# Moving the last hidden rows and weight loads one loop forward, and reordering products, silus, statistics and head sums, in an attention and expert block

## The chip, the core and the metric

The kernel runs on one core of one Trainium2 chip. Its time is the device time of one execution in microseconds (us). Matmuls run on TensorE (PE in the profile; its weight loads are PEld), elementwise work on VectorE (DVE), activations and copies on ScalarE (ACT), some sums and all indirect DMAs on GpSimd (POOL); SyncE (SP) issues most other DMAs.

## The reference, cut to what matters

The input is x, 16 batches of 512 tokens with 256 columns. Biases are left out here:

```python
xn = layernorm(x)
q, k, v = fmap(xn @ Wq), fmap(xn @ Wk), xn @ Wv      # fmap(y) = elu(y) + 1, 16 heads of 16
att = ((q @ (k.T @ v)) / (q . sum(k))) @ Wo          # by batch and head
shared = (silu(xn @ w_in_a) * (xn @ w_in_b)) @ w_out # w_in, w1: 256 -> 2 x 512
h = silu(xn @ w1_a) * (xn @ w1_b)
routed = sum(p[e] * h @ w2[e] for e in best_two(xn)) # two of 8 experts, of one group of 4
out = x + att + shared + routed
```

## The kernel before, in words

One loop handles one batch b (512 tokens, 4 tiles of 128). All its matmuls are in fp32 but those of the sorting. An order written in Python is given to a scheduler, which places the instructions of each engine. It follows the order of the code, dependencies and the buffers of the pools; `tc.keep_in_program_order`, `tc.issue_after` and `tc.high_priority` bind it further.

In loop b the kernel does the following, each named by its function:

- `front(b + 1)` projects the next batch: pk (keys and routing scores) and pq (queries) are matmuls, then come biases, the feature map (min or Relu, and Exp, L324 to L328) and the routing, many small VectorE steps.
- `summarize` makes pxk = xn.T k, 8 matmuls; `normalize(b + 2)` makes the statistics (L285, L287), the Sqrt (L289) and the normalized rows of the batch after the next, sends them to DRAM and back and transposes them to xnT. Sqrt, Exp and Silu need three different tables on ScalarE, and each change is a table load (ACT_TABLE_LOAD).
- `hidden_rows(b)` makes the rows h for the experts (tiles phr and hr) and stores them to DRAM (h_d). `hidden(b)` makes the same for the shared expert, transposed (tiles phs and hs_all). Both call `seven`: for each half u it forms two sums of products out of 7 products, Strassen's way, from four sums of tokens (`token_sums`, tile ss). A product (u, i) is one matmul of 512 columns in phr and two of 256 in phs. Products add up in three PSUM tiles a half: tall, wide and lone. Product 1 is copied to r1 (L493), 6 and 7 to b1 and b2 (L496, L499), wide after 5 is added to b2 (L500), lone after 2 to r1 (L502), wide after 3 to b1 (L505). Then silu(r1) * b1 (L503, L506) and silu(tall) * b2 (L509, L510) are the outputs. r1 and the silu of tall (sa) share the pool tag "sa" of two buffers: r1 of half 0, r1 of half 1, sa 0, sa 1, then r1 of the next call. There are six PSUM buffers "mm" and two "py".
- `key_sum(b + 1)` and `attend(b + 1)` make the sum of keys (POOL, L602; matmul pks), and divide the queries by the normalizer (qk L658, rz L660 to L664, q*rz L665). `mix(b)` makes pvk (4 matmuls), vk (L637, L642), pm and kvo.
- `gather(b)` makes po for four token tiles: 4 matmuls with hs_all and w_out, 2 with kvo and the queries. It adds po to res and stores it to h_d (L695, L696).

The loop before the last (b = 14) also begins `order`, the sorting of all tokens by their pair of experts. It is a generator, advanced by `next(steps_of_order)` at places written by hand: slots for all tokens (L712 to L753), then eight groups of marks on VectorE (L770 x_all, L775 at_tile, L779 and L783) with 8 small matmuls (pi) each. Loop 14 takes 1 + 1 + 1 + 6 steps and loop 15 8 steps in its `hidden_rows` and the last.

The last loop (b = 15) begins with `token_sums` and `hidden_rows(15)`. Only after these is the place of w1's blocks free, and 16 DMAs of 128 KB load the last four experts' weights there (L198). Then the first rows are gathered from h_d by indirect DMA (L836) in the sorted order and turned: for a pair of tiles, 12 ScalarE copies to hb (L857, behind the silu of the half), 4 transposes of 32 partitions and 3 of 128 (L863, L869) give hT. 67 sorted tiles follow, four matmuls of 512 columns each (L886, tile py), then scatters, and the output tiles of batch 15.

Of the kernel before, what the change touches and what calls it, by code (L numbers as in the profile page):

```python
# [10 lines left out]
FP = mybir.dt.float32  # L11
AF = mybir.ActivationFunctionType
ALU = mybir.AluOpType
AX = mybir.AxisListType

P = 128
# [5 lines left out]
def block_kernel(  # L22
# [29 lines left out]
    nc = tc.nc  # L52
# [196 lines left out]
    ahead_of = keep.tile([P, TT + 1, NP], BF)  # L249
    nc.gpsimd.memset(ahead_of[:, 0, :], 0.0)  # L250

    last_xn, last_copy = [], []

    def turn(to, rows, tag, b, parts):

# [12 lines left out]

        return place

    def normalize(b):

        xt = xs[b]
        st = small.tile([P, NT, 6], FP, tag="st", name=f"st_{b}")
        mv = small.tile([P, NT, 2], FP, tag="mv", name=f"mv_{b}")
        sd = small.tile([P, NT], FP, tag="sd", name=f"sd_{b}")
        rs = small.tile([P, NT], FP, tag="rs", name=f"rs_{b}")
        xn = xn_all[:, b % 2]

        n = 1 if b == 0 else NT  # L280
        made = []
        for g in range(0, NT, n):
            with tc.issue_after(last_xn[-1].ins) if last_xn else nullcontext():
                for t in range(g, g + n):
                    nc.vector.bn_stats(out=st[:, t, :], in_=xt[:, t, :])  # L285
            for t in range(g, g + n):
                nc.vector.bn_aggr(out=mv[:, t, :], in_=st[:, t, :])  # L287
            with tc.issue_after(last_copy[-1].ins) if last_copy else nullcontext():
                nc.scalar.activation(sd[:, g : g + n], mv[:, g : g + n, 1], AF.Sqrt, bias=eps_sb)  # L289
            nc.vector.reciprocal(rs[:, g : g + n], sd[:, g : g + n])  # L290
            for t in range(g, g + n):
                made.append(nc.vector.tensor_scalar(
                    xn[:, t, :], xt[:, t, :], mv[:, t, 0:1], rs[:, t : t + 1],
                    ALU.subtract, ALU.mult,
                ))
        last_xn[:] = made[-1:]
        xnT = work.tile([P, KD, S], FP, tag="xnT", name=f"xnT_{b}")
        if b < 2:
            for t in range(NT):
                pt = ps_mm.tile([P, KD, P], FP, tag="mm", name=f"pt_{b}_{t}")  # L300
                for c in range(KD):
                    nc.tensor.transpose(
                        pt[:, c, :], xn[:, t, :].rearrange("p (m c) -> p c m", c=KD)[:, c], ident
                    )
                last_copy.append(nc.scalar.copy(xnT[:, :, ts(t, P)], pt))
            return xn, xnT, None
        last_copy.clear()
        nc.sync.dma_start(out=xn_d[b % 2].rearrange("(t p) d -> p t d", p=P), in_=xn)
        return xn, xnT, turn(xnT, xn_d[b % 2], "xb", b, "(i c)")
# [9 lines left out]
    def feature_map(b, y, tag):  # L319

        low = one.tile([P, NT, D], FP, tag="low", name=f"{tag}_{b}")
        if tag == "km":
            nc.vector.tensor_scalar(low, y, 0.0, None, ALU.min)  # L323
            nc.scalar.activation(low, low, AF.Exp)  # L324
        else:
            nc.scalar.activation(low, y, AF.Relu, scale=-1.0)
            nc.scalar.activation(low, low, AF.Exp, scale=-1.0)
        nc.vector.scalar_tensor_tensor(y, y, 0.0, low, ALU.max, ALU.add)  # L328

    def project(b, xnT):  # L330
# [128 lines left out]
    def token_sums(b, xnT):  # L459

        (x11, x12), (x21, x22) = halves(xnT)
        ss = one.tile([P, 4, S // 2], FP, tag="ss", name=f"ss_{b}")
        s1, s2, s3, s4 = (ss[:, i, :] for i in range(4))
        nc.vector.tensor_tensor(s1, x21, x22, ALU.add)
        nc.vector.tensor_tensor(s2, s1, x11, ALU.subtract)
        nc.vector.tensor_tensor(s3, x11, x21, ALU.subtract)
        nc.vector.tensor_tensor(s4, x12, s2, ALU.subtract)
        return [x11, x12, s4, x22, s1, s2, s3]

    def seven(name, product, view, room, done, then):  # L470
# [11 lines left out]
            )  # L482
        r1, b1, b2 = [None] * 2, [None] * 2, [None] * 2
        for n, (u, i) in enumerate((
            (0, 1), (0, 5), (1, 1), (0, 6), (1, 5), (1, 6), (0, 7), (0, 2), (1, 7), (0, 4), (0, 3),
            (1, 2), (1, 3), (1, 4),
        )):
            to = lone[u] if i == 2 else wide[u] if i in (3, 5) else tall[u]
            product(to, u, i - 1, i in (1, 2, 5), i in (2, 3, 4))
            with tc.high_priority():  # L490
# [5 lines left out]
                    nc.scalar.copy(b1[u], view(tall[u]))  # L496
                elif i == 7:
                    b2[u] = room(u, 1)
                    nc.scalar.copy(b2[u], view(tall[u]))  # L499
                    nc.vector.tensor_tensor(b2[u], b2[u], view(wide[u]), ALU.add)  # L500
                elif i == 2:
                    nc.vector.tensor_tensor(r1[u], r1[u], lone[u], ALU.add)  # L502
                    nc.scalar.activation(r1[u], r1[u], AF.Silu)  # L503
                elif i == 3:
                    nc.vector.tensor_tensor(b1[u], b1[u], view(wide[u]), ALU.add)  # L505
                    done(u, 0, None, nc.vector.tensor_tensor(b1[u], view(r1[u]), b1[u], ALU.mult))  # L506
# [92 lines left out]
    def key_sum(b, kk):  # L599

        k2 = one.tile([P, 2, D], FP, tag="k2", name=f"k2_{b}")
        nc.gpsimd.tensor_tensor(k2, kk[:, 0:2, :], kk[:, 2:4, :], ALU.add)  # L602
        nc.gpsimd.tensor_tensor(k2[:, 0, :], k2[:, 0, :], k2[:, 1, :], ALU.add)
        pks = ps_y.tile([P, D], FP, tag="py", name=f"pks_{b}")
        nc.tensor.matmul(pks, lhsT=ones, rhs=k2[:, 0, :], start=True, stop=True)
# [14 lines left out]
        nc.scalar.copy(xk, pxk)  # L620
        return xk

    def mix(b, xk, ksb):

        pvk = ps_mm.tile([P, KD, P], FP, tag="mm", name=f"pvk_{b}")
        for c in range(KD):
            for k in range(KD):
                nc.tensor.matmul(
# [6 lines left out]
        with tc.high_priority():  # L635
            for c in range(KD):
# [5 lines left out]
            nc.vector.tensor_tensor(  # L642
                vk, vk, headmask.unsqueeze(1).to_broadcast([P, KD, P]), ALU.mult
            )
        pm = ps_mm.tile([P, KD, D], FP, tag="mm", name=f"pm_{b}")
        for c in range(KD):
            nc.tensor.matmul(
# [40 lines left out]

    def gather(b, res, qT, kvo, hs, placed, then):

        for t in range(NT):
            po = outputs(b, t, qT, kvo, hs)

            with tc.issue_after(placed.ins) if placed and t > 1 else nullcontext():
                nc.vector.tensor_tensor(res[:, t, 0:D], po, res[:, t, 0:D], ALU.add)  # L695
            nc.sync.dma_start(out=h_d[ts(b * NT + t, P), HID:ROW], in_=res[:, t, :])  # L696
            between(b, then(t))

    def order():

# [221 lines left out]
    for b in range(B):  # L922
        xn, xnT, _ = normed.pop(b)
        res, qq, kk = fronts.pop(b)
        if b + 1 < B:
            fronts[b + 1] = front(b + 1, normed[b + 1][1])
        if b + 2 == B:
# [3 lines left out]
            )  # L931
            steps_of_order = order()
        if b + 1 == B:
            sums7 = token_sums(b, xnT)
            hidden_rows(b, sums7, {2: 2, 6: 2, 9: 2, 13: 2}.get)

            for e in waiting:
                load_expert(e)
            *lists, filled = next(steps_of_order)
            tiles = [Tiles(list(range(i, min(i + 2, SURE))), *lists) for i in range(0, SURE, 2)]  # L940
        xk = summarize(b, xn, kk)
# [14 lines left out]
        if b + 1 < B:  # L956
            sums = key_sum(b + 1, fronts[b + 1][2])
            queries[b + 1] = attend(b + 1, fronts[b + 1][1], sums)
        if b + 2 == B:
            next(steps_of_order)  # L960
        if b + 1 == B:
# [1 line left out]
                w.rows()  # L963
        hs, made = hidden(b, sums7) if b else first_hidden(xnT)
        if b + 1 < B:
            kvo = mix(b, xk, ksb)
        if b + 2 == B:
            next(steps_of_order)
        if b + 1 < B:
            gather(b, res, qT, kvo, hs, normed[b + 2][2]() if b + 2 < B else None, {0: 2, 1: 2, 3: 2}.get)  # L970

# [10 lines left out]
    for g, w in enumerate(tiles):  # L982
# [3 lines left out]
            tiles[g + AHEAD - 1].turn()  # L986
        w.sums()
        if g == AHEAD:
            kvo = mix(B - 1, xk, ksb)

    def rest(i):
        if i < TILES:
# [59 lines left out]
```

## Time and profile before

| | |
|---|---|
| median of 3 runs | 1048.22 us (1044.43 to 1048.23) |
| the profiled execution | 1048.47 us, span 1046.7 us |
| TensorE busy | 1012.4 us, 3704 matmul instructions |
| mean granted TensorE clock | 0.991 |
| idle TensorE: start | 8.9 us |
| idle TensorE: ahead of the first expert tile | 8.88 us, at 786.97 to 795.85 us |
| idle TensorE: loop 14 (710 to 755 us) | 2.47, 0.23 and 1.90 us |
| ScalarE table loads in the program | 48, 1.28 us each |
| memory read and written | 63.52 and 50.27 MB |

One loop takes about 47 us. An fp32 matmul of 256 columns is two instructions in the records, and follows the one before it after 0.431 us; one of 512 columns after 0.862 us. On VectorE an instruction's record overlaps the next one by some 0.08 us, so its cost in a queue is the distance of two starts, not its length. A wait is named by what ended it. The sum of idle time and of time at a lower clock is all that can change when the matmuls stay the same.

### The profile page before, as it was taken

What the parts mean: (1) busy time and instruction counts of PE and PEld (TensorE: products, weight loads), DVE (VectorE), ACT (ScalarE), POOL (GpSimd) and SP (SyncE); (2) the same over time, 40 slices, a digit from 0 to 9 for tenths busy, and PEclk for the clock granted to TensorE, in tenths of its full rate; (3) what the DMA queues carried; (4) which work ended last, traced back from release to release, by engine and by line L of the source; (5) the groups of instructions that cost most, each with busy time, mean ns of one, the idle gap of its engine ahead of it and who ended that gap; (6) DMA issues with size and microseconds to landing.
All of it is one profiled execution on the core that took longest, in us unless ns stands there. A gap on an engine that the chain in (4) does not pass through costs nothing. (4 is left out here: it accounts for less than half of the span.)

```text
span 1046.7 us, 12393 instructions
## 1 busy us (share of the span) xinstructions
PE 1012.4 (97%) x3704; PEld 682.5 (65%) x3704; DVE 783.4 (75%) x1976; ACT 479.8 (46%) x888; POOL 246.4 (24%) x355
## 2 busy tenths in 40 slices
PE   6999999999999989999999999999896999999998
PEld 5576867778686858686777768686673444444445
DVE  6968797978879686878786777878966566666662
ACT  3425353534435352525353343425138666667770
POOL 7111011020202021120202020211022555565541
PEclk9999999999999999999999999999998999999999
DMA  8333452424253332323132323221244445554441
GB/s 237 98 95 104 122 144 57 146 61 147 67 152 107 92 101 62 119 62 121 61 101 76 96 66 101 86 61 62 60 129 139 138 141 154 151 155 146 154 124 70
DMA packets 129955, 114.23 MB, mean 109 GB/s; under 512 B 72109, under 2 KB 114109, under 8 KB 129888
## 3 DMA queue, kind: packets, MB, share of 16 engines
q1 hardware_dynamic: 119936, 77.16, 24.8%
q0 software_dynamic: 8976, 35.22, 11.2%
q10 hardware_dynamic: 976, 1.05, 0.3%
q8 instruction: 31, 0.51, 0.2%
q14 instruction: 36, 0.29, 0.1%
HBM read 63.52 MB, written 50.27 MB: 109 GB/s over the span
## 5 line engine op out<-in xcount | busy, mean ns | idle before, releaser
L886 PE MATMUL py<-w_sb,hT 128*128 x536 | 232.5, 596 | 8.9 <-DMA w_sb<-in_w 8.9
L886 PEld LDWEIGHTS py<-w_sb,hT 128*128 128x128 f32 x536 | 102.6, 192 | 137.8 <-issue 137.8
L684 PE MATMUL po<-wout_sb,hs_all 128*128 128x256 f32 x512 | 123.4, 380 | 0.7 <-PEq L993 0.4
L316 POOL TENSOR_TENSOR res<-x_all,bo_sb 128x256 f32<-128x256 f32 x64 | 52.2, 846 | 271.5 <-DVE lg L343 168.0
L684 PEld LDWEIGHTS po<-wout_sb,hs_all 128*128 128x128 f32 x512 | 95.3, 190 | 14.9 <-DVE hs_all L506 1.1
L324 ACT ACTIVATE km<-km 128x1024 f32<-128x1024 f32 x16 | 16.9, 1057 | 165.4 <-DVE km L323 165.4
L899 POOL DMA_INDIRECT out<-y,goal x67 | 67.9, 1013 | 104.0 <-DVE y L896 94.4
L695 DVE TENSOR_TENSOR res<-po,res 128x256 f32<-128x256 f32 x60 | 25.4, 424 | 76.3 <-PE po L684 76.2
L602 POOL TENSOR_TENSOR k<-kk_all 128x512 f32<-128x512 f32 x16 | 20.9, 1305 | 258.0 <-DVE sm L384 255.7
L521 PE MATMUL phr_w<-w_sb,ss 128*128 128x512 f32 x120 | 63.2, 609 | 4.6 <-DVE hr L500 2.7
L684 PE MATMUL po<-kvo,qT 128*128 128x256 f32 x256 | 66.0, 383 | 0.0
L547 PE MATMUL phs_t<-ss,win_sb 128*128 128x256 f32 x240 | 60.3, 384 | 2.9 <-ACT r_phs L493 2.9
L547 PE MATMUL phs_t<-xnT,win_sb 128*128 128x256 f32 x240 | 62.8, 379 | 0.0
L521 PE MATMUL phr_t<-w_sb,xnT 128*128 128x512 f32 x120 | 62.2, 600 | 0.0
L338 PE MATMUL pk<-wkr_sb,xnT 128*128 128x266 f32 x256 | 62.0, 396 | 0.0
L547 PE MATMUL phs_w<-ss,win_sb 128*128 128x256 f32 x240 | 61.6, 379 | 0.0
L521 PE MATMUL phr_t<-w_sb,ss 128*128 128x512 f32 x120 | 59.4, 597 | 0.1
L615 PE MATMUL pxk<-kk_all,xn_all 128*128 128x256 f32 x256 | 57.9, 379 | 0.0
L349 PE MATMUL pq<-w_sb,xnT 128*128 128x256 f32 x256 | 57.8, 379 | 0.0
L338 PEld LDWEIGHTS pk<-wkr_sb,xnT 128*128 128x128 f32 x256 | 49.8, 195 | 9.2
L684 PEld LDWEIGHTS po<-kvo,qT 128*128 128x128 f32 x256 | 47.5, 190 | 8.9 <-ACT kvo L651 3.0
L857 ACT COPY hb<-qq_all 32x256 f32<-32x256 f32 x108 | 43.4, 402 | 21.4 <-DMA qq_all<-h_d,source 15.9
(202 smaller groups left out, 1923.9 us busy)
## 6 DMA issues: line engine op xcount, KB each, us to landing
h_d<-hr SPq DMA_DIRECT2D x64, 256.0 KB
q_d<-qq_all SPq DMA_DIRECT2D x16, 512.0 KB
qb<-q_d SPq DMA_DIRECT2D x64, 128.0 KB
w_sb<-in_w SPq DMA_DIRECT2D x64, 128.0 KB
h_d<-res SPq DMA_DIRECT2D x60, 129.0 KB
x_all<-in_x SPq DMA_DIRECT2D x15, 512.0 KB
xn_d<-xn_all SPq DMA_DIRECT2D x14, 512.0 KB
xb<-xn_d SPq DMA_DIRECT2D x56, 128.0 KB
```

The lines of the kernel that those rows point to most:

```text
L316: nc.gpsimd.tensor_tensor(res[:, t, 0:D], xt[:, t, :], bo_sb, ALU.add)
L338: nc.tensor.matmul(pk, lhsT=xnT[:, k, ts(t, P)], rhs=wkr_sb[:, k, :], start=(k == 0), stop=(k == KD - 1),)
L349: nc.tensor.matmul(pq[:, t, :], lhsT=xnT[:, k, ts(t2 + t, P)], rhs=wq_sb[:, k, :], start=(k == 0), stop=(k == KD - 1),)
L521: tc.keep_in_program_order(nc.tensor.matmul(to, lhsT=xs7[i][:, ts(u, P)], rhs=w1_in[W7[i]], start=start, stop=stop, skip_group_check=True,))
L547: tc.keep_in_program_order(nc.tensor.matmul(split(to)[:, f, :], lhsT=win_in[W7[i]][:, ts(2 * u + f, P)], rhs=xs7[i], start=start and f == ...
L602: nc.gpsimd.tensor_tensor(k2, kk[:, 0:2, :], kk[:, 2:4, :], ALU.add)
L615: nc.tensor.matmul(pxk[:, c, :], lhsT=xn[:, t, ts(c, P)], rhs=kk[:, t, :], start=(t == 0), stop=(t == NT - 1),)
L684: step = nc.tensor.matmul(po, lhsT=a, rhs=w, start=(i == 0), stop=(i == len(parts) - 1))
L695: nc.vector.tensor_tensor(res[:, t, 0:D], po, res[:, t, 0:D], ALU.add)
L857: nc.scalar.copy(there[ts(q, Q), a - near, 0:n, :], self.hg[ts(a, Q), 0:n, ts(q, W)])
L886: nc.tensor.matmul(py.rearrange("p j d -> p (j d)"), lhsT=self.hT[:, f, ts(j, P)], rhs=w2_sb[:, f, bass.ds(regs[i % TR], 2 * D)], start=(f ...
L899: stored = nc.gpsimd.indirect_dma_start(out=out_rows, out_offset=bass.IndirectOffsetOnAxis(ap=self.goal[:, i : i + 1], axis=0), in_=y, in_ ...
```

## The change

No arithmetic is added or removed. It has these parts:

1. Inside `seven`, the order of the 14 products ends in (1,2), (1,4), (0,3), (1,3) where it was (0,3), (1,2), (1,3), (1,4). The silu of r1 of half 0 is now written behind the copy of product (1,7), and both are kept in program order.
2. In loop 14, `token_sums(15)`, `hidden_rows(15)` and the 16 weight loads now stand ahead of `gather(14)`; in loop 15 they are gone. The eight steps of `order` in `hidden_rows(15)` come along. The sums ss of batch 15 lie in the tag "blocks" of another pool.
3. `mix` is split: pvk and vk become `values`, called ahead of `hidden`; pvk uses a "py" buffer in loops 0 to 13.
4. The statistics become `measure`. From batch 3 on they are written at the head of loop b - 2, and Sqrt is issued after the last Exp of the queries, with high priority.
5. `key_sum` adds in two instructions of 256 columns where it was one of 512.
6. `gather` takes the token tiles in the order 2, 3, 0, 1.

By the built program, pks now stands behind the third product of phr and pvk between phr and phs on TensorE; in loops 7 to 13 most of the pk matmuls of the batch after the next stand ahead of po; ScalarE holds, per loop, Exp, then Sqrt, then the copies, then all four silus; the 12 copies to hb follow all four silus of phs_15; on SP the 16 loads stand ahead of the four stores of res_14; there are 46 table loads.

```diff
@@ -249,7 +249,7 @@
     ahead_of = keep.tile([P, TT + 1, NP], BF)
     nc.gpsimd.memset(ahead_of[:, 0, :], 0.0)
 
-    last_xn, last_copy = [], []
+    last_xn, last_copy, last_exp, measured = [], [], [], {}
 
     def turn(to, rows, tag, b, parts):
 
@@ -268,11 +268,22 @@
 
         return place
 
+    def measure(b, tiles):
+
+        if b not in measured:
+            st = small.tile([P, NT, 6], FP, tag="st", name=f"st_{b}")
+            measured[b] = st, small.tile([P, NT, 2], FP, tag="mv", name=f"mv_{b}")
+        st, mv = measured[b]
+        with tc.issue_after(last_xn[-1].ins) if last_xn else nullcontext():
+            for t in tiles:
+                nc.vector.bn_stats(out=st[:, t, :], in_=xs[b][:, t, :])
+        for t in tiles:
+            nc.vector.bn_aggr(out=mv[:, t, :], in_=st[:, t, :])
+        return mv
+
     def normalize(b):
 
         xt = xs[b]
-        st = small.tile([P, NT, 6], FP, tag="st", name=f"st_{b}")
-        mv = small.tile([P, NT, 2], FP, tag="mv", name=f"mv_{b}")
         sd = small.tile([P, NT], FP, tag="sd", name=f"sd_{b}")
         rs = small.tile([P, NT], FP, tag="rs", name=f"rs_{b}")
         xn = xn_all[:, b % 2]
@@ -280,13 +291,12 @@
         n = 1 if b == 0 else NT
         made = []
         for g in range(0, NT, n):
-            with tc.issue_after(last_xn[-1].ins) if last_xn else nullcontext():
-                for t in range(g, g + n):
-                    nc.vector.bn_stats(out=st[:, t, :], in_=xt[:, t, :])
-            for t in range(g, g + n):
-                nc.vector.bn_aggr(out=mv[:, t, :], in_=st[:, t, :])
-            with tc.issue_after(last_copy[-1].ins) if last_copy else nullcontext():
-                nc.scalar.activation(sd[:, g : g + n], mv[:, g : g + n, 1], AF.Sqrt, bias=eps_sb)
+            mv = measured[b][1] if b > 2 else measure(b, range(g, g + n))
+
+            first = last_copy or (last_exp if b > 2 else [])
+            with tc.issue_after(first[-1].ins) if first else nullcontext():
+                with tc.high_priority() if b > 2 else nullcontext():
+                    nc.scalar.activation(sd[:, g : g + n], mv[:, g : g + n, 1], AF.Sqrt, bias=eps_sb)
             nc.vector.reciprocal(rs[:, g : g + n], sd[:, g : g + n])
             for t in range(g, g + n):
                 made.append(nc.vector.tensor_scalar(
@@ -324,7 +334,7 @@
             nc.scalar.activation(low, low, AF.Exp)
         else:
             nc.scalar.activation(low, y, AF.Relu, scale=-1.0)
-            nc.scalar.activation(low, low, AF.Exp, scale=-1.0)
+            last_exp[:] = [nc.scalar.activation(low, low, AF.Exp, scale=-1.0)]
         nc.vector.scalar_tensor_tensor(y, y, 0.0, low, ALU.max, ALU.add)
 
     def project(b, xnT):
@@ -459,7 +469,11 @@
     def token_sums(b, xnT):
 
         (x11, x12), (x21, x22) = halves(xnT)
-        ss = one.tile([P, 4, S // 2], FP, tag="ss", name=f"ss_{b}")
+
+        if b + 1 < B:
+            ss = one.tile([P, 4, S // 2], FP, tag="ss", name=f"ss_{b}")
+        else:
+            ss = work.tile([P, 4, S // 2], FP, tag="blocks", name=f"ss_{b}")
         s1, s2, s3, s4 = (ss[:, i, :] for i in range(4))
         nc.vector.tensor_tensor(s1, x21, x22, ALU.add)
         nc.vector.tensor_tensor(s2, s1, x11, ALU.subtract)
@@ -482,8 +496,8 @@
             )
         r1, b1, b2 = [None] * 2, [None] * 2, [None] * 2
         for n, (u, i) in enumerate((
-            (0, 1), (0, 5), (1, 1), (0, 6), (1, 5), (1, 6), (0, 7), (0, 2), (1, 7), (0, 4), (0, 3),
-            (1, 2), (1, 3), (1, 4),
+            (0, 1), (0, 5), (1, 1), (0, 6), (1, 5), (1, 6), (0, 7), (0, 2), (1, 7), (0, 4), (1, 2),
+            (1, 4), (0, 3), (1, 3),
         )):
             to = lone[u] if i == 2 else wide[u] if i in (3, 5) else tall[u]
             product(to, u, i - 1, i in (1, 2, 5), i in (2, 3, 4))
@@ -496,11 +510,15 @@
                     nc.scalar.copy(b1[u], view(tall[u]))
                 elif i == 7:
                     b2[u] = room(u, 1)
-                    nc.scalar.copy(b2[u], view(tall[u]))
+                    tc.keep_in_program_order(nc.scalar.copy(b2[u], view(tall[u])))
                     nc.vector.tensor_tensor(b2[u], b2[u], view(wide[u]), ALU.add)
+                    if u:
+
+                        tc.keep_in_program_order(nc.scalar.activation(r1[0], r1[0], AF.Silu))
                 elif i == 2:
                     nc.vector.tensor_tensor(r1[u], r1[u], lone[u], ALU.add)
-                    nc.scalar.activation(r1[u], r1[u], AF.Silu)
+                    if u:
+                        nc.scalar.activation(r1[u], r1[u], AF.Silu)
                 elif i == 3:
                     nc.vector.tensor_tensor(b1[u], b1[u], view(wide[u]), ALU.add)
                     done(u, 0, None, nc.vector.tensor_tensor(b1[u], view(r1[u]), b1[u], ALU.mult))
@@ -599,7 +617,8 @@
     def key_sum(b, kk):
 
         k2 = one.tile([P, 2, D], FP, tag="k2", name=f"k2_{b}")
-        nc.gpsimd.tensor_tensor(k2, kk[:, 0:2, :], kk[:, 2:4, :], ALU.add)
+        for t in range(2):
+            nc.gpsimd.tensor_tensor(k2[:, t, :], kk[:, t, :], kk[:, t + 2, :], ALU.add)
         nc.gpsimd.tensor_tensor(k2[:, 0, :], k2[:, 0, :], k2[:, 1, :], ALU.add)
         pks = ps_y.tile([P, D], FP, tag="py", name=f"pks_{b}")
         nc.tensor.matmul(pks, lhsT=ones, rhs=k2[:, 0, :], start=True, stop=True)
@@ -620,9 +639,12 @@
         nc.scalar.copy(xk, pxk)
         return xk
 
-    def mix(b, xk, ksb):
-
-        pvk = ps_mm.tile([P, KD, P], FP, tag="mm", name=f"pvk_{b}")
+    def values(b, xk, ksb):
+
+        if b + 2 < B:
+            pvk = ps_y.tile([P, KD, P], FP, tag="py", name=f"pvk_{b}")
+        else:
+            pvk = ps_mm.tile([P, KD, P], FP, tag="mm", name=f"pvk_{b}")
         for c in range(KD):
             for k in range(KD):
                 nc.tensor.matmul(
@@ -642,6 +664,10 @@
             nc.vector.tensor_tensor(
                 vk, vk, headmask.unsqueeze(1).to_broadcast([P, KD, P]), ALU.mult
             )
+        return vk
+
+    def mix(b, vk):
+
         pm = ps_mm.tile([P, KD, D], FP, tag="mm", name=f"pm_{b}")
         for c in range(KD):
             nc.tensor.matmul(
@@ -688,13 +714,14 @@
 
     def gather(b, res, qT, kvo, hs, placed, then):
 
-        for t in range(NT):
+
+        for n, t in enumerate((2, 3, 0, 1)):
             po = outputs(b, t, qT, kvo, hs)
 
-            with tc.issue_after(placed.ins) if placed and t > 1 else nullcontext():
+            with tc.issue_after(placed.ins) if placed and n > 1 else nullcontext():
                 nc.vector.tensor_tensor(res[:, t, 0:D], po, res[:, t, 0:D], ALU.add)
             nc.sync.dma_start(out=h_d[ts(b * NT + t, P), HID:ROW], in_=res[:, t, :])
-            between(b, then(t))
+            between(b, then(n))
 
     def order():
 
@@ -922,6 +949,8 @@
     for b in range(B):
         xn, xnT, _ = normed.pop(b)
         res, qq, kk = fronts.pop(b)
+        if 0 < b < B - 2:
+            measure(b + 2, range(NT))
         if b + 1 < B:
             fronts[b + 1] = front(b + 1, normed[b + 1][1])
         if b + 2 == B:
@@ -931,11 +960,7 @@
             )
             steps_of_order = order()
         if b + 1 == B:
-            sums7 = token_sums(b, xnT)
-            hidden_rows(b, sums7, {2: 2, 6: 2, 9: 2, 13: 2}.get)
-
-            for e in waiting:
-                load_expert(e)
+            sums7 = last_sums
             *lists, filled = next(steps_of_order)
             tiles = [Tiles(list(range(i, min(i + 2, SURE))), *lists) for i in range(0, SURE, 2)]
         xk = summarize(b, xn, kk)
@@ -956,6 +981,7 @@
         if b + 1 < B:
             sums = key_sum(b + 1, fronts[b + 1][2])
             queries[b + 1] = attend(b + 1, fronts[b + 1][1], sums)
+            vk = values(b, xk, ksb)
         if b + 2 == B:
             next(steps_of_order)
         if b + 1 == B:
@@ -963,9 +989,14 @@
                 w.rows()
         hs, made = hidden(b, sums7) if b else first_hidden(xnT)
         if b + 1 < B:
-            kvo = mix(b, xk, ksb)
+            kvo = mix(b, vk)
         if b + 2 == B:
             next(steps_of_order)
+
+            last_sums = token_sums(b + 1, normed[b + 1][1])
+            hidden_rows(b + 1, last_sums, {2: 2, 6: 2, 9: 2, 13: 2}.get)
+            for e in waiting:
+                load_expert(e)
         if b + 1 < B:
             gather(b, res, qT, kvo, hs, normed[b + 2][2]() if b + 2 < B else None, {0: 2, 1: 2, 3: 2}.get)
 
@@ -986,7 +1017,7 @@
             tiles[g + AHEAD - 1].turn()
         w.sums()
         if g == AHEAD:
-            kvo = mix(B - 1, xk, ksb)
+            kvo = mix(B - 1, values(B - 1, xk, ksb))
 
     def rest(i):
         if i < TILES:
```

## The prediction

> **What bounds the kernel now.** I read the page's busy shares first, then TensorE's waits, then the 2 and 4 us windows around each long wait, and then the timelines there.
>
> From the page of the kernel before (engine, busy us, share, instructions):
>
> ```profile
> PE 1012.4 (97%) x3704; PEld 682.5 (65%) x3704; DVE 783.4 (75%) x1976; ACT 479.8 (46%) x888; POOL 246.4 (24%) x355
> ```
>
> TensorE is busy 1012.4 of 1046.7 us, and this change alters no matmul. So the time can only move by TensorE's idle time (34.3 us) and by its clock. TensorE's waits (what, for whom: total us, times, longest):
>
> ```profile
> PE pt L302 <- DVE xn_all L292: 8.9, 2, 8.6
> PE py L886 <- DMA w_sb<-in_w: 8.9, 1, 8.9
> PE phs_t L547 <- ACT r_phs L493: 2.9, 8, 0.8
> PE phr_w L521 <- DVE hr L500: 2.7, 3, 2.1
> PE pm L647 <- DVE rz L663: 2.5, 1, 2.5
> PE pm L647 <- DVE vk L642: 2.2, 1, 2.2
> PE phr_w L521 <- DVE ss L464: 1.9, 1, 1.9
> ```
>
> The first is the start, which the change leaves alone. The second is the wait for the last expert weights ahead of the first expert tile. The 2.5 and 1.9 stand in loop 14, where the sorting work crowds VectorE. The clock adds to this (stretch; length; PE, PEld, DVE, ACT and POOL busy; clock; DMA share; GB/s):
>
> ```profile
> 378.00:380.00 2.00, 0.28 (x1) 0.28 (x2) 2.00 (x6) 0.89 (x2) 0.00 (x0) 1.00 0.36 80
> 380.00:382.00 2.00, 2.00 (x3) 0.69 (x3) 0.84 (x6) 1.95 (x4) 0.00 (x0) 0.54 0.00 0
> 382.00:384.00 2.00, 2.00 (x6) 1.28 (x5) 1.58 (x4) 1.25 (x2) 0.00 (x0) 0.61 0.03 8
> ```
>
> After a wait of 2.05 us the clock was 0.54 and 0.61 for 4 us: 2x0.46 + 2x0.39 = 1.7 us lost. The same windows give about 1.7 after the 1.9 us wait and 2.1 after the 8.9 us wait, and nothing after the 2.47 us and the 2.17 us one: 5.5 us in all.
>
> **The weight loads (moved).** The 16 loads of 128 KB will be issued some 40 us of matmuls ahead of the first expert tile, so their 8.9 us wait goes. What is late next? The timeline before that tile (start, length, instruction):
>
> ```profile
> 790.60 3.73 ACT L857 COPY hb<-qq_all 32x256 f32<-32x256 f32 x9
> ...
> 794.37 0.45 DVE L869 STREAM_TRANSPOSE hT<-hb 128x256 f32<-128x256 f32 x1 [0.49 <-ACT hb L857]
> ...
> 795.85 6.59 PE L886 MATMUL py<-w_sb,hT 128*128 x10 [8.88 <-DMA w_sb<-in_w]
> ```
>
> TensorE's last phs product ended at 786.97; the tile hT was whole at 794.37 + 0.45 = 794.82. So without any weight load the tile would have come 7.85 us after the matmuls: of 8.88 us only 1.0 is the weights' own. The new kernel doesn't shorten this chain. Its ScalarE order has all four silus of phs_15 ahead of the 12 copies. The last silu needs the buffer that the last product r1*b1 frees, and that product now follows the last matmul pair: about 3.1 us to the end of the silus, 12 x 0.41 = 4.95 of copies, 0.45 of transpose: 8.5, of which copies may begin a little sooner. I take 8.0: a gain of 0.9 (bounds 0 to 1.5). On SP the loads now stand ahead of four res_14 stores, 16 x 0.47 = 7.5 us of issue; the gathers need these rows, but TensorE has pxk and phs (15.5 us) and the 8 us besides: 0 (bounds 0 to 2).
>
> **Loop 14 (C).** The rows of batch 15 move ahead of the 24 output matmuls of batch 14. Those had given VectorE 10.3 us of cover while it sorted. By the built program's order, VectorE does 42 instructions between the (0,3) product of phr_14 and the sum s1 that phr_15's second product reads. Their costs are starts' distances in this timeline, and in its neighbours:
>
> ```profile
> 738.85 0.19 DVE L663 TENSOR_SCALAR rz<-rz 128x64 f32<-128x64 f32 x1
> 738.95 1.22 DVE L770 TENSOR_TENSOR x_all<-count,place_of 128x1024 bf16<-128x1024 bf16 x1
> 740.08 0.54 DVE L664 RECIPROCAL rz<-rz 128x64 f32<-128x64 f32 x1
> 740.54 0.72 DVE L775 TENSOR_TENSOR at_tile<-count,place_of 128x600 bf16<-128x600 bf16 x1
> 741.18 1.21 DVE L665 TENSOR_TENSOR qq_all<-qq_all,rz 128x1024 f32<-128x1024 f32 x1
> 742.31 0.78 DVE L779 TENSOR_TENSOR qq_all<-at_tile,number 128x600 bf16<-128x600 bf16 x1
> 743.00 0.37 DVE L783 TENSOR_SCALAR qq_all<-at_tile,row 128x600 bf16<-128x600 bf16 x1
> 743.29 1.22 DVE L770 TENSOR_TENSOR x_all<-count,place_of 128x1024 bf16<-128x1024 bf16 x1
> ```
>
> 16 combinations of 512 columns at 0.60 = 9.6; vk 0.9; slots and their reductions (L731 to L753, L663) 2.6; ksb 0.3; qk, rz, its reciprocal and q*rz 1.14 + 1.13 + 0.46 + 1.13 = 3.9; three x_all marks at 1.13 = 3.4; two at_tile at 0.70, one L779 and one L783 = 2.4; s1 0.34. Sum 23.4. TensorE has between the same two points (1,3) 0.86, pks 0.43, pvk 0.86, phs 28 x 0.431 = 12.1, pm 0.86, phr_15's first product 0.86: 15.9. It will wait 23.4 + 0.2 - 15.9 = 7.7 us, in place of 2.47 + 0.23 + 1.90 = 4.6: a loss of 3.1.
>
> **The new order of products in every loop (A).** (0,3) and (1,3) now come last of 14. In the tag "sa" there are two buffers: r1 of either half, then sa of either half, then r1 of the next rows. So the copy that frees phs's first PSUM tile waits for: both L505 adds (1.20), the product r1*b1 (0.68), the silu (0.60), VectorE finishing what stands between (about 0.3), the product with sa (0.68), the copy (0.59); and in VectorE's order r1's add and the q*rz product stand ahead (0.60 + 1.22). With 0.5 to 0.7 of hand-overs that is 6.5 us from the end of (1,4). TensorE covers 5.2: (0,3), (1,3), pvk, and phs (0,1), (0,5), (1,1), 0.86 each. It waits 1.4 us at phs (0,6), in loops 1 to 13 (bounds 0.2, without q*rz in between, to 2.0): 18.2, and about 0.7 in loop 14. Before, three products more lay behind (0,3), and the row for this wait is 2.9 us in all. A loss of 16.
>
> **The outputs (B).** po needs hs, whose last silu now waits for r1*b1 of the last but one product: from the end of phs's (0,3), 0.2 + 0.69 + 0.69 + 0.60 + 0.2 + 0.68 = 3.1 against 1.72 of cover ((1,3) and pm): 1.4 us. In loops 1 to 6 po follows pm directly; from 7 on six or seven pk matmuls (2.7 to 3.1 us) stand between and cover it. 6 x 1.4 = 8.4 (bounds 2 to 13).
>
> **What costs nothing.** The statistics only change their place on VectorE (4 x 0.33 + 4 x 0.07 = 1.6 us a loop). Sqrt stands between the Exps and the silus: 46 table loads for 48, 1.28 us each, on an engine busy 46%. POOL's key sum of 1.31 us becomes two, at 0.77 by its 256-column row: +0.23 us; in loop 14 it would end near 711.6, and its matmul's turn is at 713.1. k v sums sooner take pm's 2.47 away (in C). If VectorE has no room, any of these adds its length in a loop; bounds 0 to 0.3 a loop. The 2.05 us wait in loop 7 was an add behind statistics, whose reader (0,3) now comes later; it goes, but the sums s1 are late there too: -0.6 (bounds -2 to +0.8).
>
> **The clock, by the skill and by the trace.** The Trainium skill (TensorE: Matmul & The Clock Gate, "What's actually happening") has the clock halved after an idle window of about 3.4 us. By that only C and the expert tile would lose, 2.1 each, 4.2 for 5.5: a gain of 1.3. This trace lost 1.7 us after 2.05 and after 1.9 us. I take 4.2 + 1.7 for the longer waits: +0.4; the skill speaks for keeping the bound low for the 1.4 us waits, the trace for an upper bound.
>
> **Sum.** Idle: +16 (A) + 8.4 (B) + 3.1 (C) - 0.9 (weights) - 0.6 (loop 7); clock +0.4: +26.4. Against the profiled execution's 1048.47 us this is 1074.9; the median of the runs is 1048.22, the same. Forecast: 1075.
>
> **Rivals.**
> 1. The chain of A and B doesn't bind: the two-buffer chain passes as quickly as in the row of 2.9 us, 0.3 a time. Place: every phs (0,6) and po. Then A is +1, B +1.8, the expert tile comes some 2.5 sooner; C stays +3.1: about 1049, not slower. It decides when these 19 waits average under 0.45 us. For it: the row. Against it: three products of cover are gone. 6%.
> 2. The short waits let the clock down as the 1.9 us one did: a third of 19 at 1.7 us adds 11: 1086. For it: two of the four waits near 2 us did. Against it: none under 1.9 did. 18%.
> 3. B is covered, by another order of readiness, and A nearer 1: 18.2 - 5 less and 8.4 less: 1061. 10%.
> The main case has 66%.
>
> **Numbers.** Main case alone 1066 to 1084; with rivals 2 and 3 the range is 1059 to 1090. A measurement tells 0.5% (5.2 us) from no change. Faster 0.03, same 0.03, slower 0.94.
>
> **What would show it.** TensorE's waits: no wait for w_sb before the first expert tile, but one of about 8 for hT; phs <- ACT r_phs about 19 in 13 or 14; po <- hs_all 8 in 6; phr_w <- ss 7 to 9; pm <- rz gone. Wrong if po and phs wait under 0.5 us, or the expert tile comes at once.

## The result and the profile after

The changed kernel takes 1093.07 us (median of 4 runs, 1090.86 to 1095.5), the kernel before 1046.67 us beside it (4 runs, 1044.43 to 1048.23). The ratio is 1.0446, interval 1.0425 to 1.0466: slower, as forecast, but by 46 us where 26 were forecast, and outside the range of 1059 to 1090 us. Between the two profiled executions, from which the tables below are made, the difference is 42 us. The profiled execution took 1090.86 us, with a span of 1088.9 us and a mean granted clock of 0.989.

The page of the kernel after, busy time of the engines:

```profile
PE 1015.3 (93%) x3704; PEld 685.6 (63%) x3704; DVE 784.5 (72%) x1976; ACT 478.7 (44%) x886; POOL 255.1 (23%) x371
```

TensorE's idle time is 1088.9 - 1015.3 = 73.6 us, from 34.3. TensorE's waits in the kernel after (what, for whom: total us, times, longest):

```profile
PE phs_t L565 <- ACT r_phs L507: 23.0, 14, 2.2
PE phr_w L539 <- DVE hr L514: 10.5, 8, 2.4
PE po L710 <- DVE hs_all L528: 8.9, 6, 1.9
PE py L913 <- issue: 8.5, 1, 8.5
PE phr_w L539 <- DVE ss L478: 8.1, 1, 8.1
PE pt L312 <- DVE xn_all L302: 7.1, 2, 6.7
PE pm L673 <- DVE vk L664: 2.2, 1, 2.2
```

Rows one, three, four and five are the ones that the prediction named. The second is the one that it said would go. Set against the rows of before, in the two profiled executions:

| term | forecast | measured |
|---|---|---|
| A, phs_t waits for r_phs | +16 | 23.0 - 2.9 = +20.1 |
| B, po waits for hs_all | +8.4 | +8.9 |
| C, loop 14 (phr_w for ss, pm for rz) | +3.1 | 8.1 - 2.5 - 1.9 = +3.7 |
| first expert tile | -0.9 | 8.5 - 8.9 = -0.4 |
| phr_w waits for hr ("loop 7") | -0.6 | 10.5 - 2.7 = +7.8 |
| start | 0 | 7.1 - 8.9 = -1.8 |
| small waits | 0 | +1.0 |
| clock (TensorE's busy time) | +0.4 | 1015.3 - 1012.4 = +2.9 |
| sum | +26.4 | +42.2 |

Of the 15.8 us that were missed, 8.4 lie in one row, 4.1 in A, and 2.5 in TensorE's busy time.

Where the new row comes from is read in loop 5. VectorE's timeline of the kernel after, at the end of phr (start, length, instruction):

```profile
301.00 1.23 DVE L684 TENSOR_TENSOR qk<-qq_all,ksb 128x1024 f32<-128x1024 f32 x1
302.26 1.22 DVE L686 TENSOR_REDUCE rz<-qk 128x64 f32<-128x1024 f32 x1
303.40 0.68 DVE L519 TENSOR_TENSOR r_phr<-r_phr,phr_l 128x512 f32<-128x512 f32 x1
303.99 1.28 DVE L514 TENSOR_TENSOR hr<-hr,phr_w 128x512 f32<-128x512 f32 x2
...
306.42 1.21 DVE L691 TENSOR_TENSOR qq_all<-qq_all,rz 128x1024 f32<-128x1024 f32 x1
307.55 1.28 DVE L523 TENSOR_TENSOR hr<-hr,phr_w 128x512 f32<-128x512 f32 x2
308.75 0.68 DVE L524 TENSOR_TENSOR hr<-r_phr,hr 128x512 f32<-128x512 f32 x1
```

and TensorE's timeline there (in brackets the idle time ahead of the instruction, and what ended it):

```profile
304.72 1.98 PE L539 MATMUL phr_w<-w_sb,ss 128*128 128x512 f32 x4 [1.36 <-DVE hr L514]
...
311.88 1.13 PE L565 MATMUL phs_t<-ss,win_sb 128*128 128x256 f32 x4 [1.68 <-ACT r_phs L507]
```

Before, the same work stood in another order on VectorE (loop 5 of the kernel before):

```profile
281.60 0.68 DVE L500 TENSOR_TENSOR hr<-hr,phr_w 128x512 f32<-128x512 f32 x1
...
287.29 0.41 DVE L607 COPY ksb<-pks 128x256 f32<-128x256 f32 x1
...
288.23 1.22 DVE L658 TENSOR_TENSOR qk<-qq_all,ksb 128x1024 f32<-128x1024 f32 x1
```

Before, qk starts 6.6 us after the first sum of the silu rows. After, qk and rz stand ahead of these sums, and q*rz between them. From the start of qk to that of the first row sum is 303.40 - 301.00 = 2.40 us; q*rz holds the next ones up for 307.55 - 306.42 = 1.13 us more. The sum L514 reads the PSUM tile wide that product (0,3) adds to, so TensorE waits for it at 304.72; the copy that frees phs's first tile stands behind L523 and L524, so TensorE waits again at 311.88.

These attention steps can start because pks is the fourth matmul of phr in the kernel after (loops 1 to 13). Before, it followed all 14 products in loop 5 and in half of the loops, and 12 of the 14 in the others.

### The profile page after: what moved, and what is told of

It is laid out like the page before. It is cut to its first block, busy times and chain, and to the rows that moved or that the text cites. A ratio compares the mean times of both kernels' runs of the same rounds, so it can differ in the third digit from the quotient of the medians.

```text
span 1088.9 us, 12364 instructions
## 1 busy us (share of the span) xinstructions
PE 1015.3 (93%) x3704; PEld 685.6 (63%) x3704; DVE 784.5 (72%) x1976; ACT 478.7 (44%) x886; POOL 255.1 (23%) x371
## 5 line engine op out<-in xcount | busy, mean ns | idle before, releaser
L621 POOL TENSOR_TENSOR k<-kk_all 128x256 f32<-128x256 f32 x32 | 23.1, 743 | 275.6 <-DVE sm L394 267.1
L539 PE MATMUL phr_w<-w_sb,ss 128*128 128x512 f32 x120 | 61.7, 617 | 18.6 <-DVE hr L514 10.5
L565 PEld LDWEIGHTS phs_t<-ss,win_sb 128*128 128x128 f32 x240 | 45.2, 193 | 34.5 <-ACT r_phs L507 28.7
L514 DVE TENSOR_TENSOR hs_all<-hs_all,phs_w 128x512 f32<-128x512 f32 x30 | 20.6, 688 | 62.1 <-ACT hs_all L513 62.1
```

Source lines behind the costliest of these rows:

```text
L539: tc.keep_in_program_order(nc.tensor.matmul(to, lhsT=xs7[i][:, ts(u, P)], rhs=w1_in[W7[i]], start=start, stop=stop, skip_group_check=True,))
L565: tc.keep_in_program_order(nc.tensor.matmul(split(to)[:, f, :], lhsT=win_in[W7[i]][:, ts(2 * u + f, P)], rhs=xs7[i], start=start and f == ...
L621: nc.gpsimd.tensor_tensor(k2[:, t, :], kk[:, t, :], kk[:, t + 2, :], ALU.add)
```

## The experiments

The theories, as the expectations name them. **Q**: the statistics part (measure, and Sqrt behind the last Exp) makes the scheduler put pks fourth, and with it ksb, qk, rz and q*rz ahead of the row sums on VectorE; this makes the phr waits and most of the phs waits. **P**: the new order of products makes both, as the prediction had it for phs. Every ratio is to the kernel before on the same chip.

| kernel | median us | ratio and interval | phr_w <- hr | phs_t <- r_phs | po <- hs_all |
|---|---|---|---|---|---|
| changed | 1093.1 | 1.0446 (1.0425 to 1.0466) | 10.5 | 23.0 | 8.9 |
| pks_last | 1064.4 | 1.0166 (1.0147 to 1.0185) | none | 1.3 | 9.0 |
| stats_late | 1067.6 | 1.0200 (1.0178 to 1.0223) | none | 1.2 | 13.0 |
| qk_late | 1061.0 | 1.0141 (1.0116 to 1.0166) | none | 4.1 | 9.0 |
| sqrt_free | 1065.4 | 1.0184 (1.0157 to 1.0211) | none | 1.2 | 13.0 |
| products_old | 1088.4 | 1.0391 (1.0363 to 1.0418) | 23.0 | 9.6 | none |
| pks_last_old_products | 1052.1 | 1.0053 (1.0028 to 1.0078) | 4.1 | none | 1.4 |
| pks_last_rows_late | 1058.3 | 1.0118 (1.0100 to 1.0135) | none | 1.3 | 11.2 |
| stats_alone | 1099.3 | 1.0500 (1.0479 to 1.0522) | 32.5 | 9.7 | none |
| before_stats_pks | 1049.3 | 1.0038 (1.0021 to 1.0054) | 4.7 | none | none |
| before_pks_fourth | 1080.1 | 1.0326 (1.0297 to 1.0355) | 19.0 | 16.3 | none |
| before_values | 1037.4 | 0.9912 (0.9889 to 0.9936) | 1.9 | none | none |
| before_values_fill | 1030.4 | 0.9852 (0.9835 to 0.9869) | 1.8 | none | none |

The three last columns are totals of TensorE's waits in us, from the profiled execution of each; "none" stands where the list of waits has no such row. The last column leaves out one wait of 0.3 to 0.7 us for the first loop's rows. Sums and differences below are of the medians; for runs on different chips they carry about 1 us (the ratios put them up to 1.1 us apart).

**1. pks_last: the changed kernel with pks kept behind phr.**

```diff
-        nc.tensor.matmul(pks, lhsT=ones, rhs=k2[:, 0, :], start=True, stop=True)
+        tc.keep_in_program_order(nc.tensor.matmul(pks, lhsT=ones, rhs=k2[:, 0, :], start=True, stop=True))
```

> The changed kernel, and one thing more: the matmul pks is kept in program order, so that it stands behind the 14 products of phr, as in the kernel before. Theory Q (queue): the early pks lets ksb, qk, rz and q*rz (about 4 us of VectorE) stand ahead of the adds of the silu rows; the waits phs <- r_phs (23.0 us) and phr_w <- hr (10.5 us) are theirs. Then both fall to about 2 us together and the time to 1065 us (1060 to 1070). Theory P (products, that of the prediction): the order of the products with two sa buffers makes the phs waits; then only the 10.5 us go, and the time is 1082 us (1078 to 1087). By both, po <- hs_all stays at 8 to 10 us.

1064.41 us. One matmul's place is worth 1093.07 - 1064.41 = 28.7 us. TensorE's waits of this kernel:

```profile
PE po L710 <- DVE hs_all L528: 9.0, 6, 2.1
...
PE phr_t L539 <- ACT r_phr L507: 5.0, 8, 0.9
...
PE phs_t L565 <- ACT r_phs L507: 1.3, 3, 0.6
```

The wait for hr is gone, and A fell from 23.0 to 1.3 us although the new product order is still there. P falls: the order alone doesn't make A.

**2. stats_late: the changed kernel without its part 4.** The statistics are written in `normalize` again, and Sqrt has neither its rule nor high priority. The built program has pks behind phr again in 13 of 14 loops, and behind its eighth product in loop 7.

```diff
-            mv = measured[b][1] if b > 2 else measure(b, range(g, g + n))
-            first = last_copy or (last_exp if b > 2 else [])
+            mv = measure(b, range(g, g + n))
+            first = last_copy
...
-        if 0 < b < B - 2:
-            measure(b + 2, range(NT))
```

> The changed kernel with the statistics and the Sqrt back where they were before (inside normalize, no tie to Exp). Theory Q: by the built order pks then goes back behind phr by itself, so this does the same as keeping pks last: 1067 us (1061 to 1073), phs and phr_w waits near 2 us each at most 4. Theory P: the place of the statistics is worth nothing; 1091 us (1086 to 1095) with phs waits still near 20 us.

1067.57 us, with hr's wait gone: Q. po waits 13.0 us: in loops 4 to 6, where Sqrt and its table loads stand between the silus of phs, it waits 2.72 us a time, for 1.4 in run 1.

**3. stats_alone: the kernel before with part 4 alone.** The diff is that of part 4 above, whose core is

```diff
+            first = last_copy or (last_exp if b > 2 else [])
...
+        if 0 < b < B - 2:
+            measure(b + 2, range(NT))
```

> The kernel before with the statistics part of the change alone (statistics at the head of the loop, Sqrt behind Exp with high priority). By the built order pks moves to the fourth place of phr. Theory Q: this part alone brings most of the loss: 1076 us (1068 to 1084), with phr_w <- hr as the largest wait (15 to 25 us), because the third product comes early here. Theory P: within 3 us of before, 1044 to 1050.

1099.26 us, 52 us slower than before, and more than the whole change costs. pks stands fourth here too. TensorE's waits:

```profile
PE phr_w L531 <- DVE hr L510: 32.5, 14, 4.3
PE phs_t L557 <- ACT r_phs L503: 9.7, 11, 1.5
```

Q is right in kind; the size was missed by 23 us. The longest of these waits, six of 2.8 to 4.3 us, let the clock down to 0.50. TensorE's busy time is 1028.1 us, 15.7 above that of before, and stretches at half clock account for 13.2 of these (18.7 us for 5.5).

**4. products_old: the changed kernel with the old order of products** (the silu and the two kept orders of part 1 as before, too).

```diff
-            (0, 1), (0, 5), (1, 1), (0, 6), (1, 5), (1, 6), (0, 7), (0, 2), (1, 7), (0, 4), (1, 2),
-            (1, 4), (0, 3), (1, 3),
+            (0, 1), (0, 5), (1, 1), (0, 6), (1, 5), (1, 6), (0, 7), (0, 2), (1, 7), (0, 4), (0, 3),
+            (1, 2), (1, 3), (1, 4),
```

> The changed kernel with the order of products, copies and silus of before. Theory P: phs and po waits fall to 3 and 1 us; 1066 us (1060 to 1071). Theory Q: the queue on VectorE stays, so the waits move: phs to about 10, phr_w up to about 20, po to about 1: 1084 us (1078 to 1090).

1088.40 us: Q. In the old order the early pks makes TensorE wait 23.0 us at phr and 9.6 at phs. The new order moved this to phs (10.5 and 23.0) and added po's 8.9: it gave the row sums more time and the following ones less.

**5. before_stats_pks: the kernel before with part 4, and pks kept behind phr.** It has the diffs of runs 3 and 1 together.

> The kernel before with the statistics part of the change alone, as in the run that cost 52 us, and the key sum's matmul pks kept in program order, behind the products of phr, where the kernel before has it. Theory Q (the statistics part costs because it pulls pks, and with it ksb, qk, rz and q*rz, ahead of the silu rows' sums): the loss goes almost whole, 1045 to 1053 us, the wait of phr_w for hr under 4 us in all. Theory R (the instructions of the statistics part themselves fill VectorE or ScalarE at the loop's head): most of the 52 us stay, 1070 to 1099, with phr_w's wait for hr still over 20 us.

1049.28 us. Of 52 us 49 go with one matmul put back. The statistics part itself costs about 3 us. One wait for hr is left, of 4.7 us, for the 4 at most that were expected.

**6. qk_late: the changed kernel, pks still fourth, but qk behind the rows.**

```diff
         def done(u, half, silu, product):
+            last_hr[:] = [product]
...
-        nc.vector.tensor_tensor(qk, qq, ksb.unsqueeze(1).to_broadcast([P, NT, D]), ALU.mult)
+        with tc.issue_after(last_hr[-1].ins) if last_hr else nullcontext():
+            nc.vector.tensor_tensor(qk, qq, ksb.unsqueeze(1).to_broadcast([P, NT, D]), ALU.mult)
```

> The changed kernel (1093.1 us) with one wait added: the product qk, and so the sums rz and the product q*rz behind it, is issued after the last product of the silu rows. The matmul pks stays fourth in phr on TensorE, and the copy ksb stays ahead of the rows' sums. Theory Q as worked out (some 4 us of VectorE ahead of the rows' sums, of which qk, rz and q*rz are 3.6, are the loss): as with pks behind the rows, 1062 to 1070 us, the waits phr_w for hr and phs_t for r_phs under 3 us each. Rival (the place of pks on TensorE, or the PSUM buffer it takes there, is the loss): 1088 to 1094 us, both waits as before.

1060.96 us, a little below what was expected, with pks on TensorE where the changed kernel has it. hr's wait is gone, and phs waits 4.1 us in all, more than the 3 expected but far below 23.0. So it isn't pks's place on TensorE or its PSUM buffer, but the VectorE work that it releases: qk, rz and q*rz.

**7. before_pks_fourth: the kernel before, only pks (and ksb) moved.** `hidden_rows` calls `key_sum(b + 1)` behind its third product in loops 1 to 14, and pks is kept in program order.

```diff
+        def after_product(n):
+            if n == 2 and third:
+                third()
+            between(b, then(n))
...
-            hidden_rows(b, sums7, {9: 1}.get)
+            early = []
+            hidden_rows(b, sums7, {9: 1}.get, lambda: early.append(key_sum(b + 1, fronts[b + 1][2])))
```

> The kernel before with one thing moved: the key sum's matmul pks stands fourth in phr in loops 1 to 14, where the changed kernel has it; statistics, products, rows and values as before. If the place of pks alone makes the loss, it is as large as with the statistics part alone (1099 us): 1085 to 1100 us, phr_w's wait for hr 20 to 33 us. If the place needs the statistics' instructions beside it, 1050 to 1075 us, phr_w's wait for hr 4 to 18 us. If it is harmless, within 4 us of before.

1080.12 us, between the two cases. The place alone makes 33 of the 52 us of run 3. The other 19 come with the statistics part: hr's wait is 19.0 us here and 32.5 there, TensorE's busy time 1018.2 and 1028.1 us.

**8. sqrt_free: the changed kernel, Sqrt without its rule.**

```diff
-            first = last_copy or (last_exp if b > 2 else [])
+            first = last_copy
```

> The changed kernel (1093.1 us) without the rule that Sqrt is issued after the last Exp; the statistics stay at the loop's head and Sqrt keeps its high priority. In the built program pks then stands behind all or most products of phr again, and Sqrt stands between the silus of phs in some loops, with two table loads of 1.28 us. Theory Q: the loss at phr goes, 1063 to 1070 us if the split silus cost nothing, up to 1080 if po waits for the table loads; phr_w's wait for hr under 3 us. Rival (the statistics at the loop's head crowd VectorE wherever pks stands): phr_w's wait for hr stays near 10 us, 1085 to 1095.

1065.35 us. The statistics are still written at the loop's head, hr's wait is gone, and pks stands behind phr in 13 of 14 loops: without the rule that binds Sqrt to the last Exp, pks doesn't move forward. po's 13.0 us comes again from loops 4 to 6, with the table loads between the silus of phs.

**9. pks_last_old_products: run 1 with the old order of products** (the diffs of runs 1 and 4 together).

> The changed kernel with pks kept behind the products of phr (1064.4 us) and the order of the products of before. If the new order of products is what makes po wait (9.0 us, 6 times 1.4, and phr_t's 5.0 us wait for r_phr), both go: 1064.4 - 6 to 9 = 1055 to 1059 us, po's wait for hs_all under 3 us. If po waits because the hand-over from phs to po is short whatever the order, it stays near 9 us: 1062 to 1066.

1052.10 us, 12.3 less than run 1 and 3 below what was expected. po's wait falls from 9.0 to 1.4 us, and phr_t's from 5.0 to 0.3: both belong to part 1 (order of products and silus). B is shown.

**10. pks_last_rows_late: run 1 with the silu rows and the weight loads of batch 15 back at the head of loop 15.**

```diff
-            sums7 = last_sums
+            sums7 = token_sums(b, xnT)
+            hidden_rows(b, sums7, {2: 2, 6: 2, 9: 2, 13: 2}.get)
+            for e in waiting:
+                load_expert(e)
...
-            last_sums = token_sums(b + 1, normed[b + 1][1])
-            hidden_rows(b + 1, last_sums, {2: 2, 6: 2, 9: 2, 13: 2}.get)
-            for e in waiting:
-                load_expert(e)
```

> The changed kernel with pks kept behind the products of phr (1064.4 us), and the last silu rows with the weight loads back at the head of loop 15. If the rows' early place costs 3 us (the 8.1 us wait of phr_w for ss, which goes, against about 4 us of waits in loop 14 that come back) and their loads gain 0.9 to 2 at the first expert tile (10.6 us now, 8.9 on the loads then): 1060 to 1065 us, TensorE's wait ahead of the first expert tile 8 to 9.5 us on w_sb. If the early loads were worth their 8.9 us, it would be 1068 or more.

1058.29 us, a little less than expected: moving the rows forward costs 6.1 us (5.0 by the ratios). The wait ahead of the first expert tile in this kernel:

```profile
PE py L913 <- DVE hT L896: 9.3, 1, 9.3
```

It is 10.6 us in run 1. With the loads late again, TensorE waits no longer there, and for hT, not for w_sb as expected: the early loads gain nothing.

**11. before_values: the kernel before with part 3 alone** (pvk and vk ahead of `hidden` in loops 0 to 14).

```diff
+            vk = values(b, xk, ksb)
...
-            kvo = mix(b, xk, ksb)
+            kvo = mix(b, vk)
```

> The kernel before with only pvk and vk moved ahead of phs, and no matmuls put ahead of the first expert tile (those gave 1030.4 us together). If the filled wait is worth its 8.9 us and the clock loss of about 2 behind it, this is 1040 to 1043 us, TensorE's waits of pm gone and the wait for w_sb 8 to 9 us. If the values were the larger part, 1032 to 1037 us.

1037.37 us, 9.4 faster than before. pm's wait for rz (2.5 us) and phs_t's for r_phs (2.9) are gone and TensorE's busy time is 1009.2 us for 1012.4; phr_w's wait for ss in loop 14 grew from 1.9 to 4.1 us. The rest of the difference lies mainly in the start (1.8 us) and in the wait for w_sb (1.4), and no run shows that these come from the edit. The time lies between the two cases of the expectation, next to the one in which the values are the larger part.

**12. before_values_fill: run 11, with other matmuls where TensorE waits for the first expert tile.** pvk of batch 15 is written ahead of phs, and pm and the first two tiles of po of batch 15 ahead of the expert tiles; the two po tiles stay in the "py" buffers' PSUM until they are added.

```diff
+        if b + 1 == B:
+            kvo = mix(b, vk)
+            early_po = [outputs(b, t, qT, kvo, hs) for t in range(2)]
```

> The kernel before with only the values part of the change (pvk and vk ahead of the shared rows phs), and the matmuls pm and the first two token tiles of po of batch 15 (14 matmul groups, about 8 us) put between the shared rows of batch 15 and the first expert tile, where TensorE waits 8.9 us for the last weights. If values sooner does what it says, pm's waits for rz (2.5 us) and vk (2.2 us) go; if the matmuls fill the wait, it falls to 0 to 3 us. Together 8 to 12 us less than before: 1035 to 1040 us. If the moved matmuls delay the rows' transposes or the weights, so that the wait comes back behind them, about 1043 to 1047.

1030.35 us, faster than before (ratio 0.9852) and below the 1035 to 1040 expected. TensorE's timeline around the first expert tile:

```profile
778.49 1.03 PE L654 MATMUL pm<-wo_sb,vk 128*128 128x256 f32 x4
779.35 1.92 PE L691 MATMUL po<-wout_sb,hs_all 128*128 128x256 f32 x8
781.35 1.13 PE L691 MATMUL po<-kvo,qT 128*128 128x256 f32 x4
...
785.65 14.83 PE L893 MATMUL py<-w_sb,hT 128*128 x34 [0.58 <-DVE hT L876]
```

Some 6.6 us of matmuls (778.49 to 785.07) cover the wait, of which 0.58 us is left, and the clock is 1.00 from 780 to 800 us. From run 11 this is 7.0 us less (6.3 by the ratios).

## Why the prediction was wrong in size

**The step that failed** is "What costs nothing": "The statistics only change their place on VectorE", and with it, for hr's wait, "it goes, but the sums s1 are late there too: -0.6". I had read in the built program that pks stands behind the third product of phr, but worked out only one follower of it: q*rz, ahead of A's copy. Its other followers, qk and rz (2.40 us in loop 5), stand ahead of the sums that phr's own product (0,3) waits for. That is +7.8 for -0.6. Runs 1, 6 and 8 take this wait away in three ways, and most of A with it: 28.7 us for the place of one matmul, where the prediction had nothing.

**A** was right as a place, and its size was off: 14 waits of 1.64 us on average for 13 of 1.4 and one of 0.7. Its cause was half right. I booked it on the new order of products, with q*rz as one term (1.22 us) of a chain of 6.5 us; "0.2, without q*rz in between" was the low bound. Runs 1 and 6 show that bound to be near the truth: with the attention steps away, A is 1.3 and 4.1 us in all. So without part 4 (run 2, 1.2 us) the forecast's largest term would hardly exist. With pks early and the old order A is 9.6 us (run 4): the two act together. No run holds q*rz alone back, so its share beside qk and rz is not shown. That the size came near is in part luck: in loop 5, 8.5 us pass from the end of (1,4) at 303.36 to phs (0,6) at 311.88, for the 6.5 that were summed, but 1.36 of them are spent in the new wait at (0,3), and only 1.68 are left to show at phs.

**B** was right: 8.9 us in 6 waits for 8.4 in 6, and run 9 shows it to belong to part 1. **C** was right: 8.1 us for 7.7. The full price of moving the rows is higher than the row's +3.7, 5 to 6 us in run 10.

**The weights** were right. The view that answers to the one in the prediction, in the kernel after:

```profile
832.77 4.97 ACT L884 COPY hb<-qq_all 32x256 f32<-32x256 f32 x12
...
837.94 0.45 DVE L896 STREAM_TRANSPOSE hT<-hb 128x256 f32<-128x256 f32 x1
838.46 0.50 PEld L913 LDWEIGHTS py<-w_sb,hT 128*128 128x128 f32 x2 [8.88 <-issue]
838.49 2.04 PE L913 MATMUL py<-w_sb,hT 128*128 x2 [8.51 <-issue]
```

The row of the matmul names no releaser, but the last transpose of hT ends at 837.94 + 0.45 = 838.39, 0.1 us ahead of the matmul: the wait is for hT, as long as the sum of 3.1, 4.95 and 0.45 made it.

**The clock.** TensorE's busy time rose by 2.9 us, for +0.4. Half of the time that TensorE was busy at half clock is 7.5 us after and 5.5 before, so the clock accounts for 2.0 of it; the other 0.9 is open. The windows behind the longest hr wait, of 2.36 us (stretch; length; PE, PEld, DVE, ACT and POOL busy; clock; DMA share; GB/s):

```profile
200.00:202.00 2.00, 2.00 (x4) 0.85 (x3) 1.97 (x3) 0.63 (x1) 0.00 (x0) 0.52 0.00 0
202.00:204.00 2.00, 2.00 (x12) 1.95 (x11) 1.58 (x5) 0.00 (x0) 0.00 (x0) 0.63 0.00 0
```

2 x 0.48 + 2 x 0.37 = 1.7 us, and the same again behind a 2.21 us wait at 417.55 us. Rival 2, a third of 19 waits, falls: none of the 20 waits of 1.3 to 2.0 us lowered it. The idle window of about 3.4 us that the Trainium skill gives (TensorE: Matmul & The Clock Gate, "What's actually happening") would have spared both; here the trace decides, and 2.21 and 2.36 us were enough (the last section shows when). Rivals 1 and 3 fall with A at 1.64 us. The terms given for rival 1 add up to about 1051 us, not 1049.

**What stays open.** The single steps don't add up. From before, values (-9.4), the rows (+6.1) and the statistics with pks kept (+3.2) make 0, where run 9, which has these and the parts 5 and 6 besides, is 6.1 us above before. The parts 5 and 6 were not tried alone. Nor is it shown how the statistics part adds the last 19 us of run 3; 9.9 of them are TensorE's busy time (1028.1 for 1018.2), and that the statistics too stand among the row sums is only an argument.

## What to carry to other kernels

Where a scheduler decides, compare the built order on every engine before pricing an edit, and follow every instruction that moved to all who stand behind it in its queue: here a rule on one small Sqrt released 3.5 us of VectorE work (2.40 + 1.13 in loop 5) ahead of sums that TensorE needed, and cost more than all else. A load issued sooner gains nothing while another chain ends at the same place; matmuls that are due later anyway, put into the wait, gained 6 to 7 us. And test the parts of a change alone: one part of this one was worth 9 us, and was buried under the others.

## What the runs showed of the chip

The length of a wait near 2 us doesn't settle whether the clock drops. In the kernel after, waits of 2.21 and 2.36 us did it (0.51 to 0.63 for 4 us), others of 2.11, 2.17 and 2.21 us did not; before, 1.90 and 2.05 us did it and 2.17 and 2.47 us did not. All six from 2.8 to 4.3 us in stats_alone did.

The clock records show when it does. In each of the 14 profiled executions the stretches at half clock begin whole multiples of 3.41 us apart, and all but the last, which ends with the record, are one, two or three times 3.41 us long. So the clock changes at the edges of fixed steps of 3.41 us, and what counts is how much of a wait falls into one step. Four pairs of neighbouring steps, two of before and two of after (columns as above):

```profile
735.14:738.55 3.41, 1.46 (x11) 1.21 (x9) 3.41 (x9) 1.57 (x3) 0.00 (x0) 1.00 0.00 0
738.55:741.96 3.41, 2.89 (x14) 2.58 (x15) 3.41 (x7) 0.59 (x1) 0.00 (x0) 1.00 0.00 0
...
376.74:380.15 3.41, 1.36 (x4) 0.40 (x3) 3.34 (x16) 1.32 (x3) 0.76 (x4) 1.00 0.54 125
380.15:383.56 3.41, 3.41 (x6) 1.57 (x5) 1.83 (x6) 2.92 (x4) 0.00 (x0) 0.50 0.00 0
...
616.51:619.92 3.41, 1.54 (x7) 1.39 (x8) 2.36 (x8) 2.52 (x5) 0.00 (x0) 1.00 0.74 283
619.92:623.33 3.41, 3.41 (x18) 3.00 (x17) 0.58 (x1) 1.38 (x3) 0.00 (x0) 1.00 0.67 217
...
415.12:418.53 3.41, 1.20 (x7) 0.88 (x6) 2.93 (x10) 2.36 (x4) 0.00 (x0) 1.00 0.61 233
418.53:421.94 3.41, 3.41 (x10) 2.69 (x9) 0.00 (x0) 0.59 (x1) 0.00 (x0) 0.50 0.83 272
```

TensorE is idle 1.95 us in the first step, since the wait of 2.47 us there runs over an edge, and the clock stays; with 2.05 us in one step it halves. In the kernel after, of two waits of 2.21 us one has 1.87 us in a step, and the clock stays, and the other all 2.21. Over all the executions, past the first 10 us, no step at full clock with up to 1.87 us idle was followed by half clock, every one with 2.02 us or more was, and between 1.90 and 2.01 us both happened.
